# A graph layer's neighbour product by Strassen's seven block products, on a kernel ordered by hand-written lists

## The chip, the core and the metric

The kernel runs on one core of a Trainium2 chip. A core has a matrix engine (TensorE, PE), a vector engine (VectorE, DVE), an activation engine (ScalarE, ACT), a general engine (GpSimd, POOL) and a queue engine that here issues nearly all transfers (SyncE, SP). Each engine carries out its own list of instructions strictly in order and meets the others through semaphores. The metric is the device time of one launch in microseconds (us); "before" is the median of three runs.

## The reference, cut to what matters

64 graphs (`b`) of 256 nodes with 512 features go through a neighbour layer and an attention layer, each with a residual and a layer norm. All is float32.

```python
# x: (64, 256, 512), adj: (64, 256, 256)
deg = jnp.sum(adj, axis=-1, keepdims=True)
agg = jnp.einsum('bij,bjf->bif', adj, x) / jnp.maximum(deg, EPS)
cat = jnp.concatenate([x, agg], axis=2)
out = jnp.einsum('bnf,of->bno', cat, W)          # W: (512, 1024)
x = _layernorm(x + jax.nn.relu(out), axis=-1)
...
scores = jnp.einsum('bhqd,bhkd->bhqk', q, k) * SCALE      # 8 heads of 64
attn = jax.nn.softmax(scores * (adj + adj)[:, None], axis=-1)
x = _layernorm(x + out_projection(attn @ v), axis=-1)
```

## The kernel before, in words

One graph is called a block. Its 256 nodes are two row halves `t` = 0, 1 of 128 (the partitions); its 512 features are two column halves `n` = 0, 1 of 256 (`G`). The work of a block is cut into named steps, and step `X` of block `b` is written `X:b` here:

- **L** (seven products L1 to L7): both halves of W at once, so that one 512-wide PSUM bank holds `o` (x with the first half of W) and `y` (x with the second half) side by side. They land in the tile `oy`: `oy[:, 0]` is `o`, `oy[:, 1]` is `y`. The rows `agg @ W` of the reference are thus computed as `adj @ y / deg`.
- **AY0, AY1** (lines 526 to 536): that neighbour product, `adj @ y`, one bank of 512 columns for each row half `t`, accumulated over the two halves `j` of the neighbours: four products of 128 x 128 by 512 columns. `aT` is the transposed adjacency.
- **AYa** (L542, L543): DVE adds the bank times 1/deg to `o`, then takes the relu and adds `x`. **AYb** takes statistics (DVE), **AYp** the norm's factors (POOL), **AYn** applies them (ACT).
- **Dway, Dz1, x1T**: the layer's result is written to DRAM, read back turned, and transposed by DVE.
- **Q, V, O** (seven products each): the projections. **S** (a to d): scores of two heads each; **m, M, e, f, r, n, T**: mask, maximum, exponentials, reciprocal, normalising, transposing; **Dw, Ds**: the weights to DRAM and back; **C0a to C1b**: weights times v; **c0, c1**: ACT copies the context out of PSUM.
- **lb, lp, ln, Dout**: the last norm and the output; **Drest, bo**: the residual read back, and the bias added to it by POOL.

L, Q, V and O are already products of 2 x 2 blocks done in seven block products instead of eight (Strassen's method in Winograd's order). Their left sums (`xS`, `yS`, `cS`, four each) are made by POOL (L376). Their seven products go to three PSUM banks `a`, `b`, `c`: products 1, 6, 7 and 4 are summed one after the other in bank `a`, 5 and 3 in bank `c`, 2 is alone in `b`. Between two products of a bank the sum so far is read out, by a copy (`k` steps: Lk1, Qk6 and so on, most on ACT) or by an add onto what is there already (`j` steps, on DVE, L416). A product so may not start before the read of the sum that it is added to.

A program matmul of float32 operands is two matmul instructions on PE, each with its own weight load. The PSUM has 8 banks, all in one pool (`banks`), given out in turn.

The order of the work is written out by hand, not planned: `START` lists the steps up to the third block, `END` those of the last four, and `PLAN` one turn of the loop between, where `V2+1` means step V2 of the block one ahead. A program records them in that order, and so fixes each engine's own list. While block `i` has its scores, block `i+1` has its projections, block `i+2` its neighbour layer, and block `i-1` its output projection. The neighbour steps are `AY0+2`, `AY1+2`, `AYa0+2` and so on.

Of the kernel before, what the change touches and what calls it, by code (L numbers as in the profile page):

```python
# [9 lines left out]
ALU = mybir.AluOpType  # L10
AX = mybir.AxisListType

P = 128
# [22 lines left out]
    AYb1:2 Qk1:1 Q5:1 AYa0:2 nd:0 L5:3 Vj2:1 rc:0 Ta:0 V6:1 nc:0 AYb0:2 Dwa:0 Q6:1 Qj2:1 AYp0:2 Td:0
    Vk6:1 AYp1:2 V5:1 Qk6:1 Tb:0 Dwd:0 L1:3 xS3:3 Vk5:1 yS4:1 Tc:0 Dwb:0 Qk5:1 V7:1 Dwc:0 Q7:1 AYn0:2
    AYn1:2 Q3:1 Qj7:1 Lk1:3 Vj7:1 aT:3 V4:1 deg:3 Dza:4 L6:3 Qj3:1 Dsa:0 Q4:1 Lk6:3 Lk5:3 Dsb:0 Vk4:1
    V3:1 Qk4:1 L7:3 Vj3:1 Drest:0 Dsc:0 Lj7:3 Sa:1 Dsd:0 Sd:1 ma:1 Dway:2 L3:3 Ma:1 md:1 L2:3 ea:1 bo:0
    Lj3:3 fa:1 L4:3 Md:1 Dz1:2 ra:1 Lk4:3 Sb:1 Dadj:4 na:1 Sc:1 mb:1 C0a:0 Lj2:3 fd:1 C1a:0 Mb:1 C1b:0  # L40
    C0b:0 Ta:1 c1:0 eb:1 AY1:3 x1T:2 Dwa:1 Dx:3 c0:0 mc:1 AY0:3 ed:1 yS1:2 Dzx:4 cS3:0 fb:1 O1:0 Wos4:0
    Dadj:5 O2:0 rb:1 yS2:2 aT:4 nb:1 Q1:2 Wos3:0 Mc:1 Q5:2 rd:1 yS4:2 Ok1:0 Qk1:2 AYa1:3 yS3:2 V1:2
    cS1:0 Qk5:2 Tb:1 Q6:2 cS2:0 ec:1 cS4:0 xT1:4 Dwb:1 Q3:2 AYb1:3 Vk1:2 Qk6:2 xT0:4 AYp1:3 O6:0 AYa0:3
    xS1:4 fc:1 V6:2 xS3:4 V5:2 Vk6:2 rc:1 Ok6:0 Q7:2 nc:1 O5:0 Vk5:2 nd:1 Q2:2 Ok5:0 Qj7:2 AYb0:3 O7:0
    Tc:1 AYp0:3 V7:2 xS2:4 O3:0 Oj2:0 Dwc:1 Oj7:0 Q4:2 Vj7:2 Qj3:2 Qj2:2 O4:0 Qk4:2 V3:2 Ok4:0 Oj3:0
    V4:2 AYn0:3 Td:1 Vk4:2 Sa:2 AYn1:3 Vj3:2 Dwd:1 Sc:2 ma:2 Dway:3 Sb:2 Drest:1 Dsc:1 mc:2 Sd:2 L1:4
    Dsb:1 Mc:2 lb0:0 Dsa:1 V2:2 Lk1:4 ec:2 lb1:0 L5:4 lp0:0 Dz1:3 mb:2 lp1:0 fc:2 L6:4 Dsd:1 md:2 xS4:4
    ln1:0 L2:4 Lk6:4 Ma:2 Lk5:4 Mb:2 L7:4 fa:2 ea:2 L3:4 Lj7:4 Vj2:2 ln0:0 Lj2:4 L4:4 Lj3:4 Dout:0 ra:2
    x1T:3 na:2 C0a:1 Dx:4 deg:4 yS1:3 C1a:1 bo:1 Md:2 Lk4:4 C0b:1 fb:2 C1b:1 rc:2 Ta:2 AY0:4 c1:1 c0:1
    Dwa:2 eb:2 Dzx:5 cS1:1 AY1:4 yS2:3 nc:2 rb:2 yS3:3 V1:3 cS2:1 Q5:3 ed:2 cS4:1 Tc:2 yS4:3 O1:1 Qk5:3  # L50
    Dwc:2 cS3:1 Dsa:2 Q2:3 Ok1:1 AYa1:4 Vk1:3 fd:2 O5:1 AYa0:4 Q1:3 nb:2 AYb1:4 O6:1 Qk1:3 V5:3 Ok6:1
    Tb:2 V6:3 Q3:3 Vk6:3 rd:2 Dwb:2 Qj2:3 Vk5:3 nd:2 Ok5:1 xT0:5 O7:1 Q6:3 Oj7:1 Td:2 V7:3 Qk6:3 Dwd:2
    Dsc:2 O2:1 O4:1 Qj3:3 Dsb:2 Q7:3 Oj2:1 Vj7:3 AYb0:4 O3:1 Qj7:3 AYp0:4 V4:3 xT1:5 AYp1:4 Ok4:1 Q4:3
    Vk4:3 Oj3:1 Drest:2 lb0:1 Dsd:2 lb1:1 V3:3 Qk4:3 V2:3 lp1:1 AYn0:4 Vj2:3 xS1:5 Vj3:3 ln1:1 lp0:1
    xS3:5
"""
PLAN = """
    Sa+0 AYn1+1
    Sb+0 ma+0 ln0-2 Dway+1
# [12 lines left out]
    O1-1
    L7+2 Ok1-1 rb+0 x1T+1 ed+0
    O5-1 Lj7+2 yS1+1 nb+0
    O6-1
    V2+1 Ok6-1 Lj2+2
    L4+2 Ta+0
    V1+1 xT1+3 Lk4+2 Dwa+0 fd+0
    Q1+1 deg+2 xT0+3 fc+0
    O7-1 Tb+0 xS1+3  # L80
    AY0+2 Vk1+1 yS2+1 Oj2-1 Qk1+1 Dwb+0 rc+0 Dsa+0 yS4+1 Ok5-1 Oj7-1
    AY1+2 nc+0 rd+0 cS4-1 xS3+3
    V6+1 AYa1+2 yS3+1 nd+0
    V5+1
    O4-1
    O3-1 Ok4-1 Vk6+1 Tc+0 Vk5+1
    Q6+1 Td+0 Dwc+0
    Q5+1 Qk6+1 Vj2+1 Dwd+0 AYa0+2 Drest+0 Dsb+0
    V3+1 Qk5+1
    V7+1 Vj3+1 Dadj+3 Oj3-1  # L90
    Q7+1 Vj7+1 Dsc+0
    Q3+1 Qj7+1 AYb0+2 Dsd+0
    V4+1 lb0-1 AYp0+2
    Q4+1 lb1-1 Vk4+1 lp0-1 AYn0+2 Qj3+1 lp1-1 AYb1+2
    Q2+1 Qk4+1 AYp1+2 ln1-1 Qj2+1
"""
END = """
    Dza:2 Sb:4 xS2:2 AYn1:3 Sa:4 xS4:2 mb:4 Dway:3 Sc:4 Mb:4 Sd:4 C1a:5 mc:4 fb:4 C0a:5 ma:4 ln0:6 C1b:5
    C0b:5 Dz1:3 md:4 L1:2 Ma:4 Dout:6 L2:2 Lk1:2 Dx:2 eb:4 L5:2 Dzx:1 c0:5 x1T:3 c1:5 L6:2 fa:4 cS1:5
    Mc:4 cS2:5 aT:2 O2:5 Lk6:2 bo:5 fc:4 O5:5 O1:5 Lk5:2 L7:2 ea:4 yS1:3 Ok1:5 yS2:3 L3:2 ec:4 Lj7:2  # L100
    Oj2:5 rc:4 V1:3 Lj2:2 nc:4 Lj3:2 L4:2 rb:4 Ok5:5 Md:4 O6:5 Lk4:2 Vk1:3 Q5:3 Ok6:5 fd:4 Tc:4 V6:3
    ed:4 xT1:1 Dwc:4 AY1:2 ra:4 deg:2 na:4 xT0:1 AY0:2 rd:4 xS3:1 AYa1:2 Qk5:3 yS3:3 Q1:3 cS3:5 AYa0:2
    Vk6:3 yS4:3 V5:3 Qk1:3 xS1:1 O7:5 cS4:5 Vk5:3 V7:3 Oj7:5 nd:4 xS2:1 Ta:4 Q6:3 AYb1:2 Q3:3 Qk6:3
    AYb0:2 AYp1:2 Vj7:3 AYp0:2 Td:4 nb:4 O4:5 Q7:3 Ok4:5 Dwd:4 lb1:5 Dwa:4 AYn1:2 lp1:5 V4:3 Qj7:3 Tb:4
    V3:3 Vk4:3 ln1:5 O3:5 Qj3:3 Dwb:4 AYn0:2 Q4:3 Vj3:3 Dsd:4 Oj3:5 lb0:5 Q2:3 Qk4:3 Dza:1 lp0:5 xS4:1
    ln0:5 Dsc:4 Qj2:3 Sa:3 Sb:3 ma:3 Drest:4 Sd:3 Dsb:4 Ma:3 Sc:3 Dadj:1 L1:1 mc:3 fa:3 Dway:2 Mc:3 L5:1
    Dsa:4 Lk1:1 ea:3 mb:3 Dout:5 L6:1 bo:4 ec:3 aT:1 L2:1 ra:3 Lk6:1 Mb:3 Dx:1 Lk5:1 fc:3 md:3 L7:1
# [23 lines left out]
def kernel(  # L131
# [36 lines left out]
    nc = tc.nc  # L168
# [3 lines left out]
    NT = N // P  # L172
# [609 lines left out]
```

## Time and profile before

| what | value |
|---|---|
| median of 3 runs | 3091.77 us (3089.83 to 3093.6) |
| the profiled execution's own time | 3093.68 us |
| its span, first to last instruction | 3091.9 us |
| granted PE clock, mean | 0.997 |
| one turn of the loop (three shown in the windows) | 47.50 us |
| transfers | 513.34 MB in 494103 packets, 166 GB/s on average |
| HBM | 308.55 MB read, 201.33 MB written |

A profile is one execution. The page gives for each engine its busy time, share of the span and number of instructions; then the span in 40 slices with the busy share in tenths; then the chain of work that ended last. In groups of instructions a line reads: line of the kernel, engine, operation, tile written <- tiles read, shape, count | busy us, mean ns of one | idle us before them and who ended that idle. Windows give the busy time of PE, PE's weight loads, DVE, ACT and POOL in a stretch, with the number of instructions, then the granted clock, the share of the transfer engines and GB/s. Matmuls are pipelined, so the listed length of a run of them overlaps the next; what one costs is read from start to start.

### The profile page before, as it was taken

To read this page: it belongs to the slowest core of one execution; us is meant where nothing else is said; L and a number is where in the kernel's file an instruction comes from. 1 tells how busy PE (TensorE), PEld (TensorE's weight loads), DVE (VectorE), ACT (ScalarE), POOL (GpSimd) and SP (SyncE) were. 2 spreads that over 40 slices of the span, in tenths; PEclk is the share of its full clock that TensorE was granted. 3 is DMA by queue.
4 is the path that set the end of the run, shared out by engine and by line. 5 is a ranking of instruction groups with operands and counts; after the bars stand their busy time and mean duration, and the time that the engine had idled before them with its cause. 6 is when DMAs were issued, how large, how long until landed. Compare 5 with 4: busy or idle time off the path is not lost.

```text
span 3091.9 us, 51161 instructions
## 1 busy us (share of the span) xinstructions
PE 3057.1 (99%) x17168; PEld 2262.9 (73%) x17168; DVE 2079.8 (67%) x3594; ACT 1713.5 (55%) x4995; POOL 979.9 (32%) x1677
## 2 busy tenths in 40 slices
PE   7999999999999999999999999999999999999997
PEld 4777777677777776777777777777777777777775
DVE  5666666666666666666666666667666666676674
ACT  2555555555555556555555555555555555555564
POOL 3332333332323333323233333232333333322333
PEclk9999999999999999999999999999999999999998
DMA  8466566565665665756656656557566575565665
GB/s 184 123 181 180 150 175 168 160 182 158 159 183 152 171 171 157 184 156 158 185 154 167 174 154 184 160 155 185 156 163 177 150 184 161 159 183 157 160 167 154
DMA packets 494103, 513.34 MB, mean 166 GB/s; under 512 B 113808, under 2 KB 392336, under 8 KB 493840
## 3 DMA queue, kind: packets, MB, share of 16 engines
q1 hardware_dynamic: 493264, 509.02, 61.6%
q8 instruction: 137, 2.24, 0.3%
q10 hardware_dynamic: 576, 1.05, 0.2%
q14 instruction: 126, 1.03, 0.1%
HBM read 308.55 MB, written 201.33 MB: 165 GB/s over the span
## 4 chain that ended last, share of the span: by engine, by line
PE 97%; DMA 2%; DVE 1%; POOL 0%; SPq 0%; issue 0%; ACT 0%; POOLq 0%; DVEq 0%
PE Qa L462 15%; PE La L435 14%; PE Lc L435 7%; PE pc L688 7%; PE Qc L462 7%; PE Oa L435 7%; PE AY L530 7%; PE Va L435 7%; PE Qb L462 4%; PE Oc L435 4%; PE Vc L435 4%; PE Lb L435 4%; PE sca L605 2%; PE scb L605 2%; PE scc L605 2%; PE Ob L435 2%
## 5 line engine op out<-in xcount | busy, mean ns | idle before, releaser
L478 ACT ACTIVATE qk<-Qa,bqk 128x128 f32<-128x128 f32 x768 | 218.8, 368 | 257.1 <-PE Qa L462 257.0
L451 ACT COPY oy<-La 128x512 f32<-128x512 f32 x192 | 112.3, 585 | 429.6 <-PE La L435 429.6
L516 POOL TENSOR_SCALAR mv<-mv 128x1 f32<-128x1 f32 x256 | 55.8, 218 | 915.1 <-DVE mv L511 884.2
L493 ACT COPY v<-Va 128x256 f32<-128x256 f32 x192 | 70.4, 367 | 340.9 <-PE Va L435 340.9
L376 POOL TENSOR_TENSOR cS<-cT 128x256 f32<-128x256 f32 x128 | 94.1, 735 | 460.4 <-ACT cT L704 460.4
L530 PE MATMUL AY<-oy,aT 128*128 128x512 f32 x512 | 230.8, 593 | 0.0
L503 DVE TENSOR_TENSOR h<-Oa,rest 128x256 f32<-128x256 f32 x192 | 81.4, 424 | 213.8 <-PE Oa L435 209.3
L416 DVE TENSOR_TENSOR oy<-Lc,oy 128x512 f32<-128x512 f32 x64 | 44.2, 691 | 253.8 <-PE Lc L435 248.8
L376 POOL TENSOR_TENSOR yS<-x1T 128x256 f32<-128x256 f32 x128 | 93.7, 732 | 335.0 <-DVE x1T L570 335.0
L376 POOL TENSOR_TENSOR xS<-xT 128x256 f32<-128x256 f32 x128 | 94.5, 739 | 305.3 <-DVE xT L341 273.0
L634 ACT ACTIVATE sa<-sa,nmaxa 128x256 f32<-128x256 f32 x256 | 127.0, 497 | 96.0 <-DVE nmaxa L628 92.4
L542 DVE SCALAR_TENSOR_TENSOR oy<-AY,deg,oy 128x512 f32<-128x512 f32 x128 | 94.8, 741 | 122.0 <-PE AY L530 122.0
L584 POOL TENSOR_TENSOR rest<-rest,bo_sb 128x512 f32<-128x512 f32 x128 | 159.6, 1269 | 29.3 <-DMA rest<-way 29.3
L530 PEld LDWEIGHTS AY<-oy,aT 128*128 128x128 f32 x512 | 96.9, 190 | 96.7 <-issue 91.9
L517 POOL TENSOR_TENSOR mv<-mv,neg_half 128x1 f32<-128x1 f32 x256 | 144.3, 564 | 21.3
L435 PE MATMUL La<-W,xT 128*128 128x512 f32 x256 | 122.6, 602 | 15.9 <-DMA W<-in_w0t_dram 15.9
L634 ACT ACTIVATE sb<-sb,nmaxb 128x256 f32<-128x256 f32 x256 | 128.8, 511 | 3.6 <-DVE nmaxb L628 3.6
L462 PEld LDWEIGHTS Qa<-x1T,Wq 128*128 128x128 f32 x1024 | 124.4, 192 | 6.5 <-DVE x1T L570 1.8
L634 ACT ACTIVATE sd<-sd,nmaxd 128x256 f32<-128x256 f32 x256 | 127.2, 501 | 1.7 <-DVE nmaxd L628 1.7
L634 ACT ACTIVATE sc<-sc,nmaxc 128x256 f32<-128x256 f32 x256 | 127.3, 501 | 1.4 <-DVE nmaxc L628 1.4
L462 PEld LDWEIGHTS Qa<-x1T,Wq_sums 128*128 128x128 f32 x1024 | 124.4, 192 | 3.9 <-issue 0.8
L462 PEld LDWEIGHTS Qa<-yS,Wq 128*128 128x128 f32 x1024 | 124.2, 192 | 3.6 <-issue 0.5
(151 smaller groups left out, 8305.1 us busy)
## 6 DMA issues: line engine op xcount, KB each, us to landing
zx<-in_x_dram SPq DMA_DIRECT2D x256, 128.0 KB, 3.7
x<-in_x_dram SPq DMA_DIRECT2D x256, 128.0 KB, 3.4
way<-x SPq DMA_DIRECT2D x64, 512.0 KB, 3.2
z<-way SPq DMA_DIRECT2D x256, 128.0 KB, 2.9
wsa<-sa SPq DMA_DIRECT2D x64, 512.0 KB, 2.6
wsd<-sd SPq DMA_DIRECT2D x64, 512.0 KB, 3.2
wsb<-sb SPq DMA_DIRECT2D x64, 512.0 KB, 3.0
wsc<-sc SPq DMA_DIRECT2D x64, 512.0 KB, 2.7
```

The costliest lines, as they stand in the source:

```text
L376: nc.gpsimd.tensor_tensor(part_of(s, b, [P, 4, 2, P])[:, k], left(b), right(b), op)
L435: nc.tensor.matmul(ps[:, :width].rearrange("p (m o) -> p m o", o=G), lhsT=left(k, b, c), rhs=w(WEIGHTS[k])[:, :, c], start=first and c == ...
L451: nc.scalar.copy(part_l(b, t, n), ps.rearrange("p (m o) -> p m o", m=2))
L462: nc.tensor.matmul(ps.rearrange("p (m j q) -> p m j q", m=2, j=2)[:, m, j], lhsT=wqk(WEIGHTS[k])[:, m, c, j * P : (j + 1) * P], rhs=left_y ...
L478: nc.scalar.activation(part_q(b, t, n)[:, m, j], ps.rearrange("p (m j q) -> p m j q", m=2, j=2)[:, m, j], AF.Identity, bias=bqk[:, m, c : ...
L517: nc.gpsimd.tensor_tensor(mv[:, 1:2], mv[:, 1:2], neg_half, ALU.pow)
L530: nc.tensor.matmul(ps, lhsT=held["aT", b][:, j, t], rhs=held["oy", b][:, 1, j], start=(j == 0), stop=(j == NT - 1),)
L542: nc.vector.scalar_tensor_tensor(h, held[f"AY{t}", b], rdeg, h, ALU.mult, ALU.add)
L584: nc.gpsimd.tensor_tensor(rest, rest, bo_sb, ALU.add)
L605: nc.tensor.matmul(sc(b, j)[:, t], lhsT=qk[d, 0, hp, t * P : (t + 1) * P], rhs=qk[d, 1, hp].rearrange("d (t b m) -> d b t m", t=NT, m=L), ...
L634: nc.scalar.activation(rows(b)[:, r], rows(b)[:, r], AF.Exp, bias=of("nmax", b)[:, r : r + 1], accum_out=of("total", b)[:, r : r + 1],)
L688: nc.tensor.matmul(ps[j * D : (j + 1) * D, hp % 2], lhsT=held["v", b][:, c, h * D : (h + 1) * D], rhs=held[f"sT{name}", b][:, :, c, j * NT ...
```

## The change

The neighbour product is done like L, Q, V and O: 2 x 2 blocks of adj (128 x 128) by 2 x 2 blocks of y (128 x 256), seven products (Y1 to Y7) instead of eight halves of 512 columns. POOL makes four sums of adjacency blocks (`aS`) and four of y blocks (`bS`). The products use two banks: `Ya` for 1, 6, 7 and 4, and `Ycb`, whose left half holds 5 and 3 and whose right half holds 2. Each readable sum is multiplied by 1/deg and added in place to its quarter of `o` by DVE (the seven `Yk` and `Yj` steps, line 593 of the new file); the relu and the residual are a step of their own (`AYr`, line 612). All three lists are new.

```diff
 def neighbour_steps(t):
-    @step(f"AY{t}")
-    def _(b):
-        ps = bank(f"AY{t}", b)
-        for j in range(NT):
-            nc.tensor.matmul(ps, lhsT=held["aT", b][:, j, t], rhs=held["oy", b][:, 1, j],
-                             start=(j == 0), stop=(j == NT - 1))
-    @step(f"AYa{t}")
+    @step(f"AYr{t}")
     def _(b):
         h = held["oy", b][:, 0, t]
-        rdeg = held["deg", b][:, t : t + 1]
-        nc.vector.scalar_tensor_tensor(h, held[f"AY{t}", b], rdeg, h, ALU.mult, ALU.add)
         nc.vector.scalar_tensor_tensor(h, h, 0.0, held["x", b][:, t], ALU.max, ALU.add)
...
+def small_sum(name, k, of, left, right, op):
+    steps[f"{name}{k}"] = lambda b: nc.gpsimd.tensor_tensor(of(k)(b), left(b), right(b), op)
+small_sum("aS", 1, adj_sum, adj_block(1, 0), adj_block(1, 1), ALU.add)
+small_sum("aS", 2, adj_sum, adj_sum(1), adj_block(0, 0), ALU.subtract)
+small_sum("aS", 3, adj_sum, adj_block(0, 0), adj_block(1, 0), ALU.subtract)
+small_sum("aS", 4, adj_sum, adj_block(0, 1), adj_sum(2), ALU.subtract)
+small_sum("bS", 1, y_sum, y_block(0, 1), y_block(0, 0), ALU.subtract)
+small_sum("bS", 2, y_sum, y_block(1, 1), y_sum(1), ALU.subtract)
+small_sum("bS", 3, y_sum, y_block(1, 1), y_block(0, 1), ALU.subtract)
+small_sum("bS", 4, y_sum, y_block(1, 0), y_sum(2), ALU.subtract)
+def neighbour_product(k, acc, left, right):
+    @step(f"Y{k}")
+    def _(b):
+        name = "Ya" if acc == "a" else "Ycb"
+        ps = bank(name, b) if k in (5, 1) else held[name, b]
+        nc.tensor.matmul(ps[:, G:] if acc == "b" else ps[:, :G], lhsT=left(b), rhs=right(b),
+                         start=k in (5, 1), stop=True, skip_group_check=True)
+neighbour_product(5, "c", adj_sum(1), y_sum(1))
+neighbour_product(1, "a", adj_block(0, 0), y_block(0, 0))
+neighbour_product(3, "c", adj_sum(4), y_block(1, 1))
+neighbour_product(6, "a", adj_sum(2), y_sum(2))
+neighbour_product(2, "b", adj_block(0, 1), y_block(1, 0))
+neighbour_product(7, "a", adj_sum(3), y_sum(3))
+neighbour_product(4, "a", adj_block(1, 1), y_sum(4))
+def neighbour_part(name, acc, t, n):
+    @step(name)
+    def _(b):
+        ps = held["Ya" if acc == "a" else "Ycb", b]
+        h = held["oy", b][:, 0, t, n * G : (n + 1) * G]
+        nc.vector.scalar_tensor_tensor(h, ps[:, G:] if acc == "b" else ps[:, :G],
+                                       held["deg", b][:, t : t + 1], h, ALU.mult, ALU.add)
+# Yk5 (t 1, n 1), Yk1 (0, 0), Yk6 (0, 1), Yk4 (1, 0), Yj3 (0, 1), Yj2 (0, 0), Yj7 (1, 1)
```

One turn, old and new (the lists of the first and of the last blocks are rewritten in the same way, over 100 lines):

```diff
 PLAN = """
-    Sa+0 AYn1+1
-    Sb+0 ma+0 ln0-2 Dway+1
-    Sd+0 Dzx+3 Ma+0
-    Sc+0 Dout-2
-    C0a-1 mb+0 ea+0
...
-    AY0+2 Vk1+1 yS2+1 Oj2-1 Qk1+1 Dwb+0 rc+0 Dsa+0 yS4+1 Ok5-1 Oj7-1
-    AY1+2 nc+0 rd+0 cS4-1 xS3+3
-    V6+1 AYa1+2 yS3+1 nd+0
...
-    Q4+1 lb1-1 Vk4+1 lp0-1 AYn0+2 Qj3+1 lp1-1 AYb1+2
-    Q2+1 Qk4+1 AYp1+2 ln1-1 Qj2+1
+    Sa+0 xS4+2 AYn0+1 Dout-2 Md+0
+    Sb+0 aS1+2
+    C1a-1 Dway+1 mc+0 fd+0
...
+    L7+2 Lj2+2 deg+2 fc+0
+    L3+2 Dsd+0 Ok1-1 Lj7+2 fa+0 x1T+1
+    O5-1 fb+0
+    O6-1 yS1+1
+    L4+2 Ok6-1 ec+0 Lj3+2 Ok5-1 bS1+2
+    Q1+1 Oj2-1 Lk4+2 ra+0 aS2+2 xT1+3 na+0 bS2+2 xT0+3
+    Y1+2 aS3+2
+    O7-1 Dzx+4 xS3+3
+    O3-1 Oj7-1 bS3+2 Yk1+2 Dx+2
+    Q5+1 rc+0 aS4+2 rb+0 nc+0 Oj3-1 yS3+1 Ta+0 Dza+3 yS2+1
+    V1+1 lb0-1
+    O4-1 Qk1+1 lp0-1
+    Y6+2 Ok4-1
+    Q2+1 Yk6+2 nb+0 yS4+1 Tc+0 bS4+2
+    Y5+2 Dwc+0
+    Q6+1 Yk5+2 Drest+0 Vk1+1 Dwa+0 lb1-1 Tb+0
+    Y2+2 Qk6+1
+    Y7+2
+    Y3+2 Qj2+1 Dwb+0
+    V5+1 Dadj+3 Qk5+1 Yj7+2
+    V6+1 Yj3+2 Yj2+2
+    Q7+1 AYr0+2 Vk6+1 Dsc+0 Vk5+1 Dsa+0
+    Y4+2 Qj7+1
+    V2+1 aT+3
+    V7+1 Dsb+0 Yk4+2
+    Q4+1 AYb0+2 AYr1+2 AYp0+2
+    Q3+1 Vj7+1 Qk4+1 AYb1+2 AYp1+2 ln0-1
+    V3+1 lp1-1
+    V4+1 Vj3+1 Qj3+1 Vk4+1
+    Sd+1 xS1+3 Vj2+1 AYn1+2
+    Sc+1 xS2+3 md+1 ln1-1
```

## The prediction

> **What bounds the kernel now.** I read the head of the page first, then its slices, then the share of the last chain, then three single turns by windows, then one turn's matmuls in order of time.
>
> ```profile
> span 3091.9 us, 51161 instructions
> PE 3057.1 (99%) x17168; PEld 2262.9 (73%) x17168; DVE 2079.8 (67%) x3594; ACT 1713.5 (55%) x4995; POOL 979.9 (32%) x1677
> PE   7999999999999999999999999999999999999997
> PE 97%; DMA 2%; DVE 1%; POOL 0%; SPq 0%; issue 0%; ACT 0%; POOLq 0%; DVEq 0%
> ```
>
> TensorE (PE) is busy 99% of the span and is 97% of the chain that ended last; only the first and the last slice have holes. A busy PE is not proof of a saturated one, so I look at single turns (columns: length, then busy of PE, weight loads, DVE, ACT, POOL).
>
> ```profile
> 350.00:397.50 47.50, 47.50 (x272) 35.33 (x270) 32.30 (x57) 26.74 (x79) 15.03 (x26) 1.00 0.64 172
> 1539.75:1587.24 47.49, 47.49 (x270) 35.31 (x268) 32.19 (x58) 26.73 (x78) 15.05 (x26) 1.00 0.64 167
> 3040.00:3074.00 34.00, 26.42 (x141) 17.77 (x140) 18.36 (x36) 17.47 (x47) 11.68 (x20) 0.90 0.94 248
> 3074.00:3092.00 18.00, 8.69 (x32) 6.20 (x28) 4.54 (x11) 2.21 (x3) 5.22 (x11) 0.73 0.12 30
> ```
>
> A turn takes 47.50 us early and 47.49 us late, PE without a gap at full clock: PE alone sets the turn. In the last 52 us PE is idle for 16.9 us (7.6 and 9.3), and the clock falls to 0.90 and 0.73: there latency rules. Now the order of time inside a turn (start, length, line, step, number of matmul instructions; a program matmul of these f32 operands is two).
>
> ```profile
> 1563.30 3.60 PE L530 MATMUL AY<-oy,aT 128*128 128x512 f32 x8
> 1566.74 1.03 PE L435 MATMUL Va<-Wv_sums,yS 128*128 128x256 f32 x4
> 1567.60 1.03 PE L435 MATMUL Vc<-Wv_sums,yS 128*128 128x256 f32 x4
> 1570.19 1.95 PE L462 MATMUL Qa<-yS,Wq_sums 128*128 128x128 f32 x16
> 1571.97 1.95 PE L462 MATMUL Qc<-yS,Wq_sums 128*128 128x128 f32 x16
> ```
>
> Starts count, not lengths, since the lengths overlap. Eight 512-wide matmuls take 1566.74 - 1563.30 = 3.44 us (430 ns each), four 256-wide ones 0.865 us (216 ns, by steps V and O throughout), sixteen 128-wide ones 1.785 us (112 ns).
>
> **The change part by part.**
>
> *PE.* Per block 8 matmuls of 512 columns go (3.44 us) and 7 products x 2 = 14 of 256 columns come: 7 x 0.4325 = 3.03 us, half a V step each. That saves 0.41 us a block, over 64 blocks **26.4 us**. The price of a 256-wide matmul is the only term; if the narrow ones cost per column what the 128-wide do (112/128 = 0.872 ns against 0.845), fourteen take 3.13 us and the saving is 20 us; if they cost per column what the 512-wide do, 3.01 us and 27.5 us. I take the V row, whose shape is the same, weight load included.
>
> [...]
>
> *DVE.* Two combined adds go, seven come, and the relu-and-residual pass stays (L543, now a step of its own).
>
> ```profile
> L542 DVE SCALAR_TENSOR_TENSOR oy<-AY,deg,oy 128x512 f32<-128x512 f32 x128 | 94.8, 741 | 122.0 <-PE AY L530 122.0
> L416 DVE TENSOR_TENSOR oy<-La,oy 128x512 f32<-128x512 f32 x64 | 44.2, 691 | 17.9 <-PE La L435 16.7
> L416 DVE TENSOR_TENSOR v<-Va,v 128x256 f32<-128x256 f32 x64 | 27.1, 423 | 2.9 <-ACT v L493 0.6 <-PE Va L435 0.2
> L584 POOL TENSOR_TENSOR rest<-rest,bo_sb 128x512 f32<-128x512 f32 x128 | 159.6, 1269 | 29.3 <-DMA rest<-way 29.3
> L376 POOL TENSOR_TENSOR yS<-x1T 128x256 f32<-128x256 f32 x128 | 93.7, 732 | 335.0 <-DVE x1T L570 335.0
> ```
>
> A 256-wide combined add isn't in the trace: the plain add says 423 ns at 256 and 691 at 512, so 741 - 268 = 473 ns (between 423 and 741). Seven are 3.3 us, less 2 x 0.741: +1.8 us, DVE from 32.2 to 34.0 us of a turn of 47.1. It has 13 us to spare, so this costs nothing but order.
>
> *POOL.* Eight sums come: four 256-wide at 0.732, four 128-wide, which the trace lacks; carrying the line through 1269 and 732 down one more step gives 0.46 (bounds: 0.22, the smallest POOL operation on the page, and 0.73). Together 4.8 us: POOL from 15.0 to 19.8 us. Cover again, if they are early enough.
>
> [...]
>
> *Order.* The listing shows PE's new turn: Sa Sb C1a C0a C1b C0b L1 L5 O2 L6 O1 L2 L7 L3 O5 O6 L4 Q1 Y1 O7 O3 Q5 V1 O4 Y6 Q2 Y5 Q6 Y2 Y7 Y3 V5 V6 Q7 Y4 V2 V7 Q4 Q3 V3 V4 Sd Sc. With L 1.72, Q 1.785, O, V, S and C 0.865, Y 0.43 and about 0.1 us at each change into S, C and L (read off the same turn), from Sa = 0: L1 5.4, L3 15.7, Q1 20.9, Y1 22.6, Y6 28.3, Y5 30.5, Q6 31.0, Y2 32.7, Y7 33.2, Y3 33.6, Q7 35.8, Y4 37.5, Q4 39.7, Sd 45.0. Every new wait is then a date; each engine runs its list strictly in order.
>
> - POOL: bS1 needs the join Lj3, which on DVE stands behind Lj7 (0.69), x1T (1.22) and an O join (0.42, waiting for O6's end at 19.1): 20.4. Then bS1, aS2, bS2: 22.3, due at Y6 28.3. Then aS3, xS3, bS3, aS4, yS3, yS2: 26.2, due for yS2 at Q6 31.0. Then a norm factor triple and yS4, bS4: 30.1, due 37.5. Spare: 4.8 us and more.
> - DVE reads between two products into one bank: Y1 to Y6 has 5.2 us, Y6 to Y7 4.4, Y7 to Y4 3.9; Y5 to Y2 (one tile) 1.8. A read starts about 0.2 us after its product and takes 0.47. The tightest is Yk5 before Y2: DVE reaches it at 31.2 behind a 1.23 us transpose, done 31.65, due 32.7: **1.1 us spare**. Next come Qk6 before Q7, Qj7 before Q4 and Qj3 before Sa, 1.3 to 1.4 us each.
> - SP: the three last score transfers are issued from about 36 to 41 us and needed from 48.9; in the trace of before a 512 KB score write lands in 2.6 to 3.2 us.
>
> So I put the steady turn at 47.50 - 0.41 = 47.09 us with no stall.
>
> *Head.* The first two blocks have little other work for PE, and there products follow each other into one bank: Y7 right behind Y3 and Y2 then Y4 in block 0, Y6 then Y7 in block 1. Each waits for an add (0.47 + 0.2, less 0 to 0.4 of other products): +1.5 us, bounds 0 and +4.
>
> *Tail.* Between block 63's neighbour products and its first Q product the new list has 21.9 us of PE steps where the trace has 35.1 us (2983.94 to 3019.09); adds, statistics, factors, normalising, the two transfers and the transpose need about 13.5 of them at least (1.2 + 0.9 + 1.3 + 0.8 + 3.2 + 1.9 of issuing + 2.9 + 1.25). So block 63's attention starts earlier against the remaining work and more work is left beside its latency. From that Q product on, my layout of ACT's list gives 70 to 75 us to the end where the trace has 72.8; the start itself moves 3 to 4 us closer. I take -2 us; bounds -10 (over half of the 16.9 us of idle) and +8 (a worse order, by the 6 us landing of the last score transfer and one more transpose and exponential).
>
> *Sum.* Against the profiled execution: 3093.68 - 26.4 + 1.5 - 2 = 3066.8. It lies 1.9 us above the median of the runs (3091.77), so for the median **3064.9, say 3064 us** with PE as bound.
>
> **The rivals.**
>
> 1. *A small wait appears each turn.* If the DVE list reaches Yk5 1.35 us later than laid out, Y2 waits 0.25 us, 57 turns give back 14 us: 3078. For it: the spare is a sum of a dozen estimated dates. Against: in the turns shown DVE and ACT read L's, Q's, V's and O's banks between products all the time, and PE has no gap.
> 2. *The gain isn't there.* The seven narrow products, each behind its own wait, take as long as the wide ones (0.06 us more per product): 3091. For it: Q's 128-wide matmuls cost 4% more per column. Against: steps V and O, equally broken up, keep 0.865 us all through the turn.
> 3. *POOL becomes the bound, slower than before.* In the head Wv's first sum took 2.35 us where Wo's took 1.27, a factor 1.85. If all sums beside a busier DVE slowed like that, the nine sums from bS1 to yS2 (6 x 0.73 + 3 x 0.46 = 5.8) would end at 20.4 + 5.8 x 1.85 = 31.1 us: just due at Q6. From that factor on it decides; at 2.0, Q6 starts 1.1 us late, 0.7 us a turn net, 57 turns +39 us: 3130. Against: POOL's 256-wide rows all lie within 727 and 749 ns.
> 4. *The tail gains its full bound*: 3054.
>
> **How the numbers follow.** Forecast (3057 to 3072) 0.66; rival 1 0.16; rival 2 0.05; rival 3 0.06; rival 4 0.07. The range 3056 to 3080 takes the forecast, rival 1 with its bound and the 20 us bound of the narrow matmul. A measurement tells 0.2% (6 us) from no change: faster (under 3085.6) 0.66 + 0.16 + 0.07 = 0.89, same 0.05, slower 0.06.
>
> **What would show it.** A turn in the middle of 47.09 us with PE busy throughout shows the main step; L571 products starting 0.43 us apart where two stand together show the price; DVE near 34 and POOL near 20 us a turn the side costs; a gap on PE ahead of Y2 or Q6 would be rival 1 or 3. I am wrong if the middle turn stays at 47.4 or more, or if the last 52 us hold over 25 us of idle PE.

## The result and the profile after

| | before | after | ratio |
|---|---|---|---|
| median, run on the same chip | 3091.18 us (4 runs, 3089.83 to 3093.6) | 3068.86 us (4 runs, 3068.5 to 3069.55) | 0.9927 [0.991, 0.9944] |
| run again later | 3090.87 us (15 runs) | 3069.1 us (5 runs, 3068.87 to 3073.0) | 0.993 [0.9917, 0.9942] |
| profiled execution, time and span | 3093.68, 3091.9 us | 3068.5, 3066.7 us | |
| one turn of the loop | 47.50 us | 47.09 us | |

22.3 us faster, 0.7%. The forecast was 3064 us in a range of 3056 to 3080.

The page of the kernel after: instructions, busy times by engine, PE's 40 slices, and the chain that ended last.

```profile
span 3066.7 us, 53019 instructions
PE 3030.1 (99%) x17552; PEld 2323.7 (76%) x17552; DVE 2144.6 (70%) x3914; ACT 1689.7 (55%) x4995; POOL 1288.0 (42%) x2189
PE   7999999999999999999999999999999999999997
PE 97%; DMA 2%; DVE 1%; ACT 0%; SPq 0%; issue 0%; POOL 0%; POOLq 0%; DVEq 0%; ACTq 0%
```

PE is still the chain, at 97%, and still full outside the first and last slice. So the place to look for the gain is what PE has to do in a turn. The windows of the kernel after (three turns; then the last 67 us in two pieces):

```profile
352.94:400.03 47.09, 47.09 (x277) 36.27 (x278) 33.29 (x62) 26.31 (x78) 19.91 (x34) 1.00 0.65 169
1530.13:1577.22 47.09, 47.09 (x276) 36.27 (x278) 33.28 (x62) 26.32 (x78) 19.90 (x34) 1.00 0.62 168
2518.97:2566.05 47.08, 47.08 (x276) 36.26 (x278) 33.27 (x62) 26.33 (x78) 19.90 (x34) 1.00 0.66 169
3000.00:3050.00 50.00, 41.66 (x252) 29.03 (x250) 29.69 (x53) 29.32 (x89) 14.95 (x24) 0.96 0.77 211
3050.00:3067.00 17.00, 8.19 (x28) 6.17 (x28) 4.54 (x11) 2.21 (x3) 4.96 (x10) 0.70 0.12 31
```

Each turn is one whole loop period; in it PE's busy time equals the length of the window, so there is no gap. VectorE (third figure in the list of engines) has 33.3 us and GpSimd (fifth) 19.9.

The price of a product, in PE's order of time (start, length, line, step). Read starts, not lengths:

```profile
1512.26 1.95 PE L475 MATMUL Qa<-yS,Wq_sums 128*128 128x128 f32 x16
1514.04 0.60 PE L571 MATMUL Ycb<-oy,aT 128*128 128x256 f32 x2
1514.48 0.59 PE L571 MATMUL Ya<-yB,aS 128*128 128x256 f32 x2
1514.91 0.59 PE L571 MATMUL Ycb<-oy,aS 128*128 128x256 f32 x2
```

Three products stand together (Y2, Y7, Y3) and start 0.44 and 0.43 us apart. The tightest date was the addition Yk5 on VectorE, which must be over before Y2:

```profile
1512.46 0.48 DVE L593 SCALAR_TENSOR_TENSOR oy<-Ycb,deg,oy 128x256 f32<-128x256 f32 x1 [0.58 <-PE Ycb L571]
```

It ends at 1512.94 and Y2 starts at 1514.04: 1.10 us to spare, as laid out. The new groups on VectorE and GpSimd (count | busy us, mean ns):

```profile
L593 DVE SCALAR_TENSOR_TENSOR oy<-Ya,deg,oy 128x256 f32<-128x256 f32 x256 | 119.5, 467 | 9.0 <-PE Ya L571 8.2
L593 DVE SCALAR_TENSOR_TENSOR oy<-Ycb,deg,oy 128x256 f32<-128x256 f32 x192 | 86.5, 476 | 39.9 <-PE Ycb L571 39.9
...
L553 POOL TENSOR_TENSOR yB<-oy 128x256 f32<-128x256 f32 x128 | 94.6, 739 | 131.7 <-DVE oy L429 126.4 <-DVE totalb L715 5.0 <-DVE totalc L715 0.2
L553 POOL TENSOR_TENSOR aS<-aT 128x128 f32<-128x128 f32 x128 | 60.1, 470 | 7.8 <-DVE aT L354 7.8
```

The estimates were 473, 732 and 460 ns.

**Where the 25.2 us of the span went.** Cut each trace where the scores of block 5 and of block 58 begin. Up to the first cut PE has 42 instructions more than before (7 blocks times 14 - 8) and none else; behind the second 24 more (4 blocks).

| | before | after | difference | of it products, -0.41 a block | rest |
|---|---|---|---|---|---|
| opening, to the scores of block 5 | 301.2 | 302.1 | +0.9 | -2.9 | **+3.8** |
| 53 turns | 2517.3 | 2495.6 | -21.7 | -21.7 | 0.0 |
| closing, from the scores of block 58 | 273.4 | 268.9 | -4.5 | -1.6 | **-2.9** |

The turn carries the gain. The opening gave some back: PE is idle for 19.6 us in it where it was 16.7. Two of the new waits are the products behind their bank's read that were counted beforehand (0.67 us each), but the largest are three on score transfers (0.52, 0.61 and 1.28 us), which nobody counted. In the closing PE is idle for 17.0 us where it was 18.1, and its granted clock is at half for 13.4 us where it was for 16.5.

### The profile page after: what moved, and what is told of

Its sections match the earlier page's. It is cut to its first block, busy times and chain, and to the rows that moved or that the text cites. A ratio compares the mean times of both kernels' runs of the same rounds, so it can differ in the third digit from the quotient of the medians.

```text
span 3066.7 us, 53019 instructions
## 1 busy us (share of the span) xinstructions
PE 3030.1 (99%) x17552; PEld 2323.7 (76%) x17552; DVE 2144.6 (70%) x3914; ACT 1689.7 (55%) x4995; POOL 1288.0 (42%) x2189
## 4 chain that ended last, share of the span: by engine, by line
PE 97%; DMA 2%; DVE 1%; ACT 0%; SPq 0%; issue 0%; POOL 0%; POOLq 0%; DVEq 0%; ACTq 0%
PE Qa L475 15%; PE La L448 15%; PE Qc L475 7%; PE pc L757 7%; PE Oa L448 7%; PE Lc L448 7%; PE Va L448 7%; PE Qb L475 4%; PE Ya L571 4%; PE Lb L448 4%; PE Oc L448 4%; PE Vc L448 4%; PE Ycb L571 3%; PE scd L674 2%; PE Ob L448 2%; PE Vb L448 2%
## 5 line engine op out<-in xcount | busy, mean ns | idle before, releaser
L529 POOL TENSOR_SCALAR mv<-mv 128x1 f32<-128x1 f32 x256 | 76.9, 301 | 773.7 <-DVE mv L524 760.1
L720 ACT ACTIVATE sc<-sc,totalc 128x256 f32<-128x256 f32 x256 | 109.2, 498 | 106.4 <-DVE totalc L715 106.4
L727 DVE STREAM_TRANSPOSE sd<-sd 128x1024 f32<-128x1024 f32 x64 | 79.6, 1244 | 110.2 <-ACT sd L720 110.2
L553 POOL TENSOR_TENSOR yB<-oy 128x256 f32<-128x256 f32 x128 | 94.6, 739 | 131.7 <-DVE oy L429 126.4
L429 DVE TENSOR_TENSOR oy<-Lb,oy 128x512 f32<-128x512 f32 x64 | 44.2, 690 | 141.9 <-PE Lb L448 135.2
L448 PE MATMUL Lb<-W,xT 128*128 128x512 f32 x256 | 122.2, 600 | 15.1 <-DMA W<-in_w0t_dram 15.1
L475 PEld LDWEIGHTS Qc<-yS,Wq_sums 128*128 128x128 f32 x1024 | 124.3, 192 | 3.3
```

The costliest lines, as they stand in the source:

```text
L448: nc.tensor.matmul(ps[:, :width].rearrange("p (m o) -> p m o", o=G), lhsT=left(k, b, c), rhs=w(WEIGHTS[k])[:, :, c], start=first and c == ...
L475: nc.tensor.matmul(ps.rearrange("p (m j q) -> p m j q", m=2, j=2)[:, m, j], lhsT=wqk(WEIGHTS[k])[:, m, c, j * P : (j + 1) * P], rhs=left_y ...
L553: steps[f"{name}{k}"] = lambda b: nc.gpsimd.tensor_tensor(of(k)(b), left(b), right(b), op)
L720: nc.scalar.activation(rows(b)[:, r], rows(b)[:, r], AF.Identity, scale=of("total", b)[:, r : r + 1])
```

## The experiments

The theory: PE alone sets the time. A product of 256 columns costs 0.43 us, each block has one product's worth less, and what the change puts on VectorE and GpSimd comes early enough. The rivals: the gain comes from the new orders of all the other work; the sums on GpSimd already cost something; narrow products have a price that the wide ones don't show. All kernels but those named are the changed kernel with one edit. Turn and cuts are those of the table above; 47.09 us, 302 and 269 us are the values to compare with. The ratio is to the kernel before, run beside each on the same chip.

| edit | median us | against before | turn us | opening, closing us |
|---|---|---|---|---|
| new lists, old products | 3097.34 | 1.0017 [1.0008, 1.0027] | 47.50 | 308, 269 |
| no sums | 3069.62 | 0.9924 [0.991, 0.9939] | 47.09 | 302, 269 |
| six products | 3041.47 | 0.9835 [0.9815, 0.9854] | 46.66 | 299, 267 |
| products of 128 columns | 3077.03 | 0.995 [0.9938, 0.9963] | 47.19 | 303, 269 |
| products side by side | 3142.65 | 1.0162 [1.0141, 1.0182] | 48.41 | 306, 270 |
| late Yk5 | 3086.36 | 0.9984 [0.9975, 0.9993] | 47.37 | 306, 270 |
| sums twice | 3076.0 | 0.9948 [0.9936, 0.9961] | 47.09 | 309, 269 |
| wide sums three times | 3179.93 | 1.028 [1.0263, 1.0298] | 48.59 | 327, 278 |
| all sums three times | 3371.23 | 1.0897 [1.0882, 1.0913] | 51.66 (50.2 to 53.1) | 340, 281 |
| the same, yS sums first | 3098.78 | 1.0023 [1.0014, 1.0033] | 47.09 | 327, 274 |
| score transfers first | 3068.73 | 0.9923 [0.991, 0.9937] | 47.09 | 303, 270 |
| unaltered, once more | 3069.1 | 0.993 [0.9917, 0.9942] | 47.09 | 306, 269 |

### Orders without Strassen

The steps Y3 and Y4 do the old wide products, Yj3 and Yk4 the old wide additions; the sums and the other Y steps are empty.

```diff
-    small_sum("aS", 1, adj_sum, adj_block(1, 0), adj_block(1, 1), ALU.add)
...
-    neighbour_product(5, "c", adj_sum(1), y_sum(1))
...
+    whole_product("Y3", 0)
+    whole_product("Y4", 1)
+    whole_part("Yj3", 0)
+    whole_part("Yk4", 1)
```

> The new lists, but the neighbour product as before: the eight 512-wide matmuls a block, one row half in the place of Y3 and one in the place of Y4, two combined adds, no sums on POOL. My theory (PE is the bound in the turn, and only its matmul columns count): the turn goes back to 47.50 us (47.09 + 0.41), the whole to 3068.9 + 26.4 - 1 = about 3094 us, no faster than the kernel before. The rival (the new orders brought the gain, the seven products little): a turn near 47.1 us and under 3080 us.

Its turn is 47.50 us, to the hundredth that of before. The lists alone bring nothing in the turn, cost 7 us in the opening and save 4 us in the closing (one profile each); the whole came 3 us above the 3094 expected. Its opening has waits on score transfers too (0.34, 0.51, 1.11 and 1.06 us) where the kernel before has none: they come with the lists, not with the seven products. The lists are there to make the dates of the new steps, and the gain is the arithmetic's.

### What a product costs

Six in place of seven:

```diff
-neighbour_product(3, "c", adj_sum(4), y_block(1, 1))
+steps["Y3"] = lambda b: None
```

> The changed kernel without the third of the seven products (its add reads the bank as the fifth product left it), so the result is not the right one and only the time is read. My theory (a 256-wide f32 product costs PE 0.4325 us a block, and nothing else takes the room it leaves): a turn of 46.66 us, the whole 27.7 us shorter, about 3041 us. The rival (another engine or a chain of waits is just behind PE): a turn of 46.9 us or more, 3055 us or more.

3041.47 us; the turn falls by 0.43 us, the price read from the starts. And the seven in half the width:

```diff
-            nc.tensor.matmul(
-                ps[:, G:] if acc == "b" else ps[:, :G],
-                lhsT=left(b),
-                rhs=right(b),
-                start=k in (5, 1),
...
+            half = ps[:, G:] if acc == "b" else ps[:, :G]
+            for c in (slice(0, P), slice(P, G)):
+                nc.tensor.matmul(
+                    half[:, c],
+                    lhsT=left(b),
+                    rhs=right(b)[:, c],
+                    start=k in (5, 1) and c.start == 0,
...
```

> Each of the seven products is issued as two matmuls of 128 columns in place of one of 256: 28 in place of 14 per block, the same arithmetic and banks. Theory (the price of a product goes with its columns, and a matmul of 128 columns takes 0.112 us beside 0.216 for 256): 14 x (2 x 0.112 - 0.216) = 0.11 us more per block, 64 x 0.11 = 7 us: 3074 to 3077 us, turn 47.20. Rival (narrow matmuls are dear here because each new weight load shows): weights are loaded 14 times more per block, at 0.1 us each 1.4 us a block, 90 us: over 3150 us.

The turn grows by 0.105 us for 14 more instructions with their weight loads, 6.7 us over 64 blocks (span +7.1, median +8). Half the width costs 3.5% more here (0.105 us on 3.03), the added weight loads included; of the 1.4 us a block that the rival gave these loads nothing shows. The 4% that rival 2 of the prediction builds on is there, and it is worth 0.1 us a turn at half this width.

### Whether the sums cost

The products read plain blocks, and none of the eight sums is made (the result is then another matrix; the shapes are the same):

```diff
-neighbour_product(6, "a", adj_sum(2), y_sum(2))
+neighbour_product(6, "a", adj_block(0, 0), y_block(1, 1))
...
```

> The changed kernel without POOL's eight sums a block; the seven products read plain blocks instead, so the neighbour product is not the right one and only the time is read. My theory (POOL's 4.8 us a turn lie beside PE's work): a turn of 47.09 us, the whole at 3066 to 3069 us, at most 1.5 us gained in the first two blocks. The rival (the sums cost something in every turn): 3060 us or less.

3069.62 against 3068.86 us, and the same turn: the sums are hidden altogether. How much room there is was tried by issuing them more often:

```diff
-        steps[f"{name}{k}"] = lambda b: nc.gpsimd.tensor_tensor(of(k)(b), left(b), right(b), op)
+        def f(b):
+            for _ in range(2):
+                nc.gpsimd.tensor_tensor(of(k)(b), left(b), right(b), op)
+        steps[f"{name}{k}"] = f
```

> GpSimd issues each of its eight sums twice, with the same result: 8 more instructions and 4.8 us more of GpSimd in each turn (19.9 to 24.7 us of 47.09). Theory (the product on TensorE is all that the time depends on, GpSimd runs ahead): its closest date is yS2, done 5.1 us before the Q products' sixth product reads it; the sums issued ahead of it in the turn delay it by about 3.6 us. So no wait: turn 47.09 us, span 3066 to 3069 us, median 3068 to 3071. [...]

The turn is as expected, 47.09 us with 4.8 us more on GpSimd (VectorE stays at 33.3 us a turn), yet the time is 7.1 us longer, which the theory did not say. It is in the opening (309.5 against 302.1 us): blocks 0 and 1 have little other work before their products, and PE waits eight times for these sums, 5.8 us in all, seven of them there (5.2 us). The rest of the difference was not separated from the waits on score transfers. "Hidden" was a statement on the turn, and the expectation took it for the whole kernel.

> GpSimd issues each of its eight sums three times, with the same result: 9.6 us more of GpSimd in each turn (29.5 us of 47.09). With the sums issued twice yS2 was done 1.07 us before the Q products' sixth product (Q6), after 5.11 us in the changed kernel: 4.04 us used up. Theory (the order of GpSimd's queue decides, not its load): yS2 now comes 2.97 us behind that product's date, TensorE waits 3.0 us there and loses 0.1 us more in starting again, turn 50.1 to 50.2 us, 57 turns x 3.1 = 177 us, with 14 us for the opening (7 us by the sums issued twice, doubled) about 3260 us, 3235 to 3270. Rival (GpSimd at 63% of the turn has room enough): turn 47.09 us, 3083 us.

It is over 100 us slower than expected. The wait is where it was named and as long, but what comes behind it is slow. PE's order, one turn:

```profile
1611.29 0.60 PE L575 MATMUL Ycb<-yB,aS 128*128 128x256 f32 x2
1614.70 3.68 PE L475 MATMUL Qa<-yS,Wq_sums 128*128 128x128 f32 x16 [2.82 <-POOL yS L389]
1618.18 0.64 PE L575 MATMUL Ycb<-oy,aT 128*128 128x256 f32 x2
```

From its start to that of the next, Q6 takes 3.48 us; in the kernel after it takes 1.78. The windows of the same kernel: 3 us behind the wait, then this turn and the one before it:

```profile
1615.00:1618.00 3.00, 3.00 (x16) 3.00 (x16) 0.00 (x0) 0.00 (x0) 2.77 (x5) 0.50 0.95 381
...
1578.78:1630.58 51.80, 48.98 (x275) 37.80 (x274) 33.41 (x62) 26.32 (x78) 29.33 (x51) 0.97 0.58 153
1528.59:1578.78 50.19, 47.36 (x276) 36.19 (x275) 33.42 (x62) 26.32 (x78) 29.36 (x51) 1.00 0.61 158
```

The granted clock (third column from the end) is 0.50 behind the wait. In the turn of 50.19 us it stays at 1.00: that turn is 47.09 + 3.1, the wait and the start alone, as expected. Of the 53 turns 8 are like that, 38 take 51.5 to 51.9 and 7 take 53.0 to 53.1. The clock's fall costs the others another 1.3 to 2.9 us.

Behind waits of 2.8 us the clock fell so in 45 turns of 53. The trace shows which turns these are. All changes of the granted clock in this run lie on one grid of 3.413 us. Cut at this grid, the wait of the turn shown and that of a turn that kept its clock read (length, PE busy, granted clock):

```profile
1611.43:1614.84 3.41, 0.59 (x4) 1.00 0.77 217
1614.84:1618.26 3.42, 3.42 (x17) 0.50 0.98 375
...
1922.05:1925.46 3.41, 1.47 (x12) 1.00 0.48 158
1925.46:1928.87 3.41, 2.52 (x19) 1.00 0.95 304
```

The first wait lies in one period, which is idle for 0.83 of its length, and the next period runs at half. The second is split, 0.57 and 0.26 of two periods, and the clock stays. So it goes in all 53 turns: the larger share was 0.66 to 0.83 in the 38 turns with one slow period, 0.57 or 0.58 in the 7 with two (where the rest of the wait, 0.25, lies in the first slow period), and 0.56 to 0.58 in the 8 that kept their clock. In this run the fall of the clock went with the place of the wait on the grid, with the border near 0.57.

Whether a short wait does it too was the last run, with the four wide sums three times and the narrow ones twice:

> GpSimd issues its four wide sums (bS) three times and its four narrow ones (aS) twice, with the same result. Against the sums all issued twice, three wide sums of 0.81 us come ahead of yS2, which then lies 2.43 - 1.07 = 1.36 us behind the date of the Q products' sixth product. With all sums issued three times TensorE waited 2.8 to 3.0 us there, and in most turns the product behind the wait ran at half speed: turns of 50.2 us (the wait alone) and of 51.5 to 53.1 us. Theory (a short wait costs only itself and 0.1 us to start again; the clock falls after the long ones alone): turn 47.09 + 1.36 + 0.1 = 48.55 us everywhere, granted clock over 0.99, time 3155 to 3170 us (57 turns x 1.47 = 84 us, opening 7 to 11 us). Rival (every wait lowers the clock): turns over 49.5 us, clock below 0.98, time over 3215 us.

```profile
1574.09 0.60 PE L575 MATMUL Ycb<-yB,aS 128*128 128x256 f32 x2
1575.93 2.05 PE L475 MATMUL Qa<-yS,Wq_sums 128*128 128x128 f32 x16 [1.25 <-POOL yS L389]
1577.82 0.60 PE L575 MATMUL Ycb<-oy,aT 128*128 128x256 f32 x2
```

Y5 and Q6 now start 1.84 us apart (0.43 without a wait), and Q6 to Y2 is 1.89 (1.78): 1.41 us lost at the wait (PE is idle for 1.25 of them) and 0.11 us of starting again. Every turn takes 48.6 us: the wait costs itself, and the granted clock stays at 1.00 in it. The idle time fills at most 0.37 of one period of the grid. The total is 10 us above the expectation: opening and closing are 33 us longer together, where 7 to 11 and four turns' waits (6 us) were allowed; in the opening the clock falls four times (granted clock of the whole run 0.995, in the kernel after 0.998).

### The order of GpSimd, not its load

The same sums three times, but the sums that Q6 needs go ahead of the neighbours':

```diff
-    O6-1 yS1+1
+    O6-1 yS1+1 yS3+1 yS2+1
...
-    Q5+1 rc+0 aS4+2 rb+0 nc+0 Oj3-1 yS3+1 Ta+0 Dza+3 yS2+1
+    Q5+1 rc+0 aS4+2 rb+0 nc+0 Oj3-1 Ta+0 Dza+3
```

> The sums issued three times as in the kernel beside it, so the same load on GpSimd, but in the turn's order GpSimd's sums of the Q products (yS3, yS2) stand directly behind yS1, ahead of all but the first of the neighbours' sums; the opening and closing lists are as they were. Theory (the order of GpSimd's queue decides): yS2 is done some 7 us earlier, the neighbours' sums 1.5 us later, of which the nearest (bS2 before product 6, aS4 before product 3) have about 0.4 and 0.0 us left: turn 47.1 to 47.5 us, and with 14 us for the opening 3083 to 3105 us. Rival (the load on GpSimd decides): as slow as the kernel beside it, turn over 49.5 us, over 3220 us.

From 51.66 to 47.09 us a turn, and 272 us off the time, with the same instructions on GpSimd and two names moved. The engine is busy for 1893 and 1908 us in all. What was missed in the turn was one date in a strictly ordered list. Outside the turns the load still costs: 3098.78 against 3068.86 us, all of it in the opening and the closing.

### The wait at the bank

All seven products stand together, in the order of their banks (Y1 Y5 Y6 Y3 Y2 Y7 Y4), each with its addition behind it, and are gone from their own lines:

```diff
-    Y1+2 aS3+2
+    aS3+2
...
+    Y1+2 Yk1+2 Y5+2 Yk5+2 Y6+2 Yk6+2 Y3+2 Y2+2 Y7+2 Yj7+2 Yj3+2 Yj2+2 Y4+2 Yk4+2
+    Qk6+1
```

> The changed kernel, but in the loop's turn the seven products stand next to each other, in the order 1 5 6 3 2 7 4, in the place of product 2, each with its add close behind it on DVE; first and last blocks as they were. My theory (each product that is added to a bank must wait out DVE's read of it; in the first blocks, where they stand so, two products 0.43 us long start 1.26 us apart): the group takes 1.26 x 3 + 0.43 = 4.2 us instead of 3.03, 1.2 us a turn, 57 turns make 67 us: about 3136 us, slower than before. The rival (the waits hide behind the weight loads or are shorter than that): under 3090 us.

```profile
1549.70 0.60 PE L571 MATMUL Ya<-oy,aT 128*128 128x256 f32 x2
1550.13 0.59 PE L571 MATMUL Ycb<-yB,aS 128*128 128x256 f32 x2
1550.87 0.70 PE L571 MATMUL Ya<-yB,aS 128*128 128x256 f32 x2
1551.41 0.59 PE L571 MATMUL Ycb<-oy,aS 128*128 128x256 f32 x2
1551.84 0.59 PE L571 MATMUL Ycb<-oy,aT 128*128 128x256 f32 x2
1552.27 0.59 PE L571 MATMUL Ya<-yB,aS 128*128 128x256 f32 x2
1553.54 0.67 PE L571 MATMUL Ya<-yB,aT 128*128 128x256 f32 x2 [0.67 <-DVE oy L593]
```

The last two add to one bank with a read between and start 1.27 us apart in place of 0.43; the third product starts another 0.31 us late, and behind each of these two waits another 0.1 us is lost. That makes 1.32 us a turn, 75 us in all, and the kernel is slower than before. So seven products for eight were a gain here only with other products between them; of the ways to put them side by side this order alone was tried.

One read late by itself, Yk5 behind two other steps of VectorE:

```diff
-    Q6+1 Yk5+2 Drest+0 Vk1+1 Dwa+0 lb1-1 Tb+0
+    Q6+1 Drest+0 Vk1+1 Dwa+0 lb1-1 Tb+0 Yk5+2
```

> On VectorE the addition of product 5 (Yk5) is moved behind one normalization's statistics (lb1) and one attention transpose's copy (Tb); nothing else is changed. In the changed kernel Yk5 ends 1.10 us before product 2 (Y2) adds to the same bank. The two steps moved ahead of it take about 2.5 us, so Yk5 would end some 0.3 to 1.5 us after product 2 could start. Theory (the wait at the bank counts as soon as the 1.1 us are used up): TensorE waits 0.3 to 0.6 us in front of product 2 in each turn, turn 47.4 to 47.7 us, time 3086 to 3103 us, that is, the whole gain of the change is lost. Rival (the addition has more room than the dates say): turn 47.09 us and 3069 us.

PE's order of this kernel at that place:

```profile
1522.81 1.95 PE L475 MATMUL Qa<-yS,Wq_sums 128*128 128x128 f32 x16
1524.77 0.70 PE L571 MATMUL Ycb<-oy,aT 128*128 128x256 f32 x2
1525.31 0.59 PE L571 MATMUL Ya<-yB,aS 128*128 128x256 f32 x2
```

Q6 to Y2 is 1.96 us (1.78 after) and Y2 to Y7 0.54 (0.43 or 0.44): 0.28 us a turn, just under the expected 0.3, and 17 of the 22 us are gone. PE's busy share hides this wait: the profile shows no idle time here, only a longer distance between starts. Rival 1 of the prediction did not happen, but it was 1.1 us away and its price, 14 us for 0.25 us, was right.

### The opening

Three steps of SyncE's queue change places in the opening list (words between them left out):

```diff
-    Dwd:0 Dsb:0 Vk4:1
+    Dwd:0 Dsb:0 Dsd:0 Vk4:1
...
-    L7:3 Mb:1 Dsd:0 L3:3
+    L7:3 Mb:1 L3:3
...
-    Dadj:5 O4:1 Yj3:4
+    O4:1 Yj3:4
...
-    AYr0:4 Drest:2 Q4:3
+    AYr0:4 Q4:3
...
-    Qk4:3 Dsb:2 lb1:1
+    Qk4:3 Dsb:2 Drest:2 Dadj:5 lb1:1
```

> The changed kernel with three DMA steps moved in SyncE's queue in the opening list alone: block 0's transfer of scores d (Dsd) goes directly behind that of scores b, the loading of adjacency block 5 (Dadj) and the reloading of weights (Drest) of block 2 go behind block 2's four score transfers. Theory (the opening lost 2.4 us to three waits of TensorE on score transfers, at 128, 211 and 213 us, because of where these stand in SyncE's queue): the waits shrink to under 0.8 us in all and the span falls from 3066.7 to about 3065, the median to 3066 to 3067.5. Rival (the transfers themselves are slow there, or what is gained is lost at the next wait): span 3066.7 within 0.4 us.

The three waits of 2.4 us became one of 0.98 at the transfers and a new one of 0.76 us at 135.7 us: the products behind the scores come earlier, and one meets the read of its bank. Its first two products were also 1 us slower (last section). The median is that of the changed kernel (3068.73 against 3068.86 and 3069.1 us). No gain: the waits moved rather than went, and what was left is below what one and the same kernel varies by:

> The changed kernel once more, unaltered, for a second profile: how far the opening and the closing of one and the same kernel differ from profile to profile. Theory (the turn is fixed, the opening and the closing vary by 1 to 2 us): turn 47.09 us again; the first score product between 71.8 and 73.2 us (71.77 before), the closing behind the last score product between 61.8 and 63.6 us (62.5 before); span 3066 to 3069 us. Rival (the profile repeats to within 0.3 us): the three waits on score transfers of 0.52, 0.61 and 1.28 us come again at the same places and the span is 3066.7 us.

The turn is 47.09 us again. The first score product (72.7 us) and the closing from the start of block 63's scores (62.8) lie within the bounds, but the span is 3071.2 us, outside them: its opening is 4.2 us longer than in the first profile. PE's order of this second profile at the same three products:

```profile
210.54 1.03 PE L757 MATMUL pc<-sTa,v 128*64 128x256 f32 x8
213.20 1.08 PE L757 MATMUL pc<-sTd,v 128*64 128x256 f32 x8 [1.63 <-DMA sTd<-wsd]
215.44 1.98 PE L757 MATMUL pc<-sTb,v 128*64 128x256 f32 x8 [1.16 <-DMA sTb<-wsb]
217.35 3.78 PE L448 MATMUL La<-W,xT 128*128 128x512 f32 x4
220.92 2.17 PE L448 MATMUL Lc<-W_sums,xS 128*128 128x512 f32 x4
```

The two waits are 0.9 us longer together (they leave 0.59 of one period of the clock's grid idle, 0.31 at most in the first profile), and behind them the clock falls: the products that took 1.02 and 1.82 us in the first profile take 1.91 and 3.57. Windows of the second profile, then of the first, over the same 5 us:

```profile
215.00:220.00 5.00, 4.56 (x11) 2.03 (x12) 1.87 (x2) 0.58 (x1) 1.88 (x3) 0.50 0.77 241
```

```profile
215.00:220.00 5.00, 5.00 (x17) 2.58 (x14) 2.01 (x3) 3.24 (x7) 4.01 (x5) 1.00 0.59 211
```

A transfer that landed a microsecond later here made the opening some 3 us longer still. So a comparison of single profiles of this kernel says nothing below 5 us, while its turns repeat to a hundredth.

## Why the prediction was right, and where its sizes were off

- *PE is the bound, and the products are the only large term.* Right: 47.50 to 47.09 us over 53 turns, 0.41 us a block as forecast. The old products under the new lists give 47.50, and one product less gives another 0.43. The narrow-price bound (20 us) and rival 2 fall by the turn itself.
- *VectorE 34.0 and GpSimd 19.8 us a turn, hidden.* 33.3 and 19.9 us, hidden: no sums, and the same time. VectorE was taken 0.7 us too high, without effect.
- *GpSimd's spare of 4.8 us and more, closest at Q6.* yS2 was done 5.1 us before Q6. Twice the sums used up 4.0 us and cost the turn nothing; 2.4 us more made PE wait 1.4 us, at Q6, the place that rival 3 named. What rival 3 lacked is the clock: with waits of 2.8 us the price was half as much again.
- *1.1 us spare at Yk5.* 1.10 us, and rival 1's wait came when Yk5 was put late.
- *Head +1.5 us (bounds 0 and +4).* Mis-sized: +3.8 in the first profile, +8.0 in the second. The two reads between products of one bank were counted; the waits on score transfers, which the new opening list brought, were not, and their price depends on the clock. By the medians, which lean on no single profile, opening and closing together cost 3.9 us (22.3 gained of 26.2), where -0.5 was forecast.
- *Tail -2 us (bounds -10 and +8).* -2.9 us; rival 4 (its full bound) did not come. The path was right too: with the products and the opening taken out, block 63's first Q product came some 5.5 us earlier (3 to 4 forecast), and from it to the end it took 75.5 us (70 to 75 forecast, 72.8 before).
- *The sum.* With the measured sizes 3093.7 - 26.2 + 3.8 - 2.9 = 3068.4 against 3068.5 us for the profiled execution. The forecast of 3064 is 4.9 us low: 1.7 by the sum (3066.8), mostly the head; 1.9 by the step from the profiled execution of before to the median, which was carried over though the profiled execution after has no such distance (3068.5 against 3068.86, the remaining 0.4); 0.9 by rounding 3064.9 to 3064. The distance of one execution from a median was chance, not a property of the kernel.

What rival 3 feared of a busier VectorE, the trace of the kernel before shows for one kind of pass alone, the one with two SBUF inputs. Where a GpSimd sum of 256 columns started during the relu-and-residual pass (L543, on `oy` and `x`), eight times and only in the opening and the closing, it took 1.17 to 1.18 us in place of 0.73, and once, during a sum of two blocks of Wq (L238), 1.70. All the others, whatever VectorE ran at their start, took 0.71 to 0.75 us. One of the eight:

```profile
57.70 0.98 DVE L543 SCALAR_TENSOR_TENSOR oy<-oy,x 128x512 f32<-128x512 f32 x1
58.10 1.18 POOL L376 TENSOR_TENSOR yS<-x1T 128x256 f32<-128x256 f32 x1
```

In no turn, before or after, did such a sum run beside that pass (L543, L612), and the sums of the turns stayed at 0.71 to 0.76 us. Rival 3's 2.35 us for Wv's first sum looks like the same: at that moment (49.34 us) VectorE ran a sum of Wq with two SBUF inputs, for 1.21 us. It was no sign of what a merely busier VectorE does.

What stays open: the new lists with the old products had +7 us in the opening and -4 in the closing, so both changes are most likely the lists' own, but openings of one and the same kernel differ by 4 us, and no run parts these sizes further.

## What to carry to other kernels

On an engine that is busy throughout, as PE is here (0.41 us a block for the change, 0.43 for one product), the gain of dropping work is the dropped work's own duration, read from start to start in the trace, times its count; the rest of the estimate is a list of dates, one for each new reader or writer on the engines beside it. Load said little about those dates: with the same instructions on GpSimd the turn was 47.1 or 51.7 us by the place of two of them. A cover that holds in the steady turn need not hold in the first blocks (5.2 us of waits there with the sums issued twice, none in the turn), so the opening is costed by itself.

## What the runs showed of the hardware

- A float32 matmul took 430, 216 and 112 ns for 512, 256 and 128 columns, start to start, with a weight load for each; a load takes 192 ns by itself in the group list, and at 128 columns the starts stay 112 ns apart.
- After a wait in the turn PE lost 0.10 to 0.11 us more in starting again (0.54 for 0.43, 1.89 for 1.78).
- The granted clock changed on a grid of 3.413 us. Waits of 1.25 us in the turn never lowered it (at most 0.37 of a period idle), waits of 2.8 us did in 45 turns of 53 (0.57 to 0.83), and two waits of 1.63 and 1.16 us with one product between them did too (0.59). In the turns the loss came to 1.3 to 2.9 us each time.
- A GpSimd sum of 256 columns that started while VectorE ran its pass with two SBUF inputs took 1.17 to 1.18 us in place of 0.73 in the kernel before.
- At the start of the program the first two products run slowly as well, and by differing amounts: first the kernel after, then the one with the score transfers first.

```profile
15.07 3.75 PE L448 MATMUL Lb<-W,xT 128*128 128x512 f32 x4 [15.07 <-DMA W<-in_w0t_dram]
18.62 1.98 PE L448 MATMUL La<-W,xT 128*128 128x512 f32 x4
20.44 1.88 PE L448 MATMUL Lc<-W_sums,xS 128*128 128x512 f32 x4
```

```profile
15.38 3.75 PE L448 MATMUL Lb<-W,xT 128*128 128x512 f32 x4 [15.38 <-DMA W<-in_w0t_dram]
18.93 2.98 PE L448 MATMUL La<-W,xT 128*128 128x512 f32 x4
21.75 1.88 PE L448 MATMUL Lc<-W_sums,xS 128*128 128x512 f32 x4
```

The first takes 3.55 us to the next start where 1.72 is usual, the second 1.82 in one run and 2.82 in the other: 1 us between two runs with the same first steps. A window over them shows a granted clock of 1.00, because the trace's clock records only begin with the step to full clock: at 18.82 us in the first run and at 21.14 in the second, 3.7 and 5.8 us after the first product starts. An estimate from the usual 1.72 us: half speed up to these records and full speed from there gives the second product 1.82 us in the first run and 2.82 in the other, as in the rows.
